# A recommender kernel on one core: a four-group layout, the history loop written out, and a reordered head

## The chip, the core and the metric

The kernel runs on one core of a Trainium2 chip. The core has five instruction streams: TensorE (PE) for matrix products, VectorE (DVE), ScalarE (ACT), GpSimd (POOL) and SyncE (SP). Here GpSimd issues gathers, and SP and ScalarE issue plain transfers. The metric is the device time of one execution in microseconds (us); less is better.

## The reference

The model scores 16384 users. Each has an item, a category and a history of 200 items.

```python
B, L, D = 16384, 200, 64
u = u_emb[user]; it = i_emb[item]; c = c_emb[cate]
h = i_emb[hist]                                   # L x B x D, a gather of 3.3 million rows
feat = concat([h, it, h - it, h * it], axis=-1)   # 256 features
a = dice(feat @ au_W1 + au_b1, au_alpha, axis=1)  # 36 units, statistics over the users of one l
w = a @ au_W2 + au_b2                             # one weight for each l and user
cur = sum(w * h, axis=0)                          # B x 64
z = concat([u, it, c, cur], axis=-1)
z = dice(z @ W1 + b1, alpha1, axis=0)             # 80 units
z = dice(z @ W2 + b2, alpha2, axis=0)             # 40 units
return z @ W3 + b3                                # 2 outputs

def dice(x, alpha, axis):
    p = sigmoid((x - mean(x, axis)) * rsqrt(var(x, axis) + 1e-8))
    return x * (p + alpha * (1.0 - p))
```

## The kernel before

**Splitting the product.** `feat @ au_W1` is taken apart by the four blocks of W1: a part that depends on the history row alone (`blk_h`), a part of the item alone (`blk_i`, with the bias), and the part of the product h * it (`blk_m`). The first is worked out once for all 100000 rows and stored beside them in DRAM (`table`, 128 floats a row); the second once for all users (`xi`). Only the third is a matrix product in the main work.

**Start.** 384 gathers of single columns of indices fetch the item, user and category rows into four `land` buffers (`fetch_one`, `keep_one`). Between them 49 blocks of table rows are loaded, transposed, multiplied and stored (`table_rows`, `table_store`). The order of `keep_one` and the blocks is written out by hand. After that the weights of the head are loaded, ten `land` buffers and both `hx` buffers are zeroed, and the ring of 12 `land` buffers starts.

**Main steps.** A step k handles 2048 users of one history position l; there are 8 steps to an l and 1600 in all. `manual_schedule` keeps the instructions of each engine in the order in which the code calls them. In step k:

- `fetch(k)` issues 16 indirect transfers on GpSimd (L202), each fetching 128 table rows of 512 bytes into `land[k % 12]`, and one transfer of `xi` on SP (L369).
- ScalarE works the gates of step k-10 (L448, L451) into the PSUM tile `pg`.
- `turn(k-1)` transposes both halves of the landed rows with four VectorE instructions (L377), and ScalarE copies one half to PSUM (L454).
- `hidden(k-2)` adds the product to the transposed table half (L390) and takes statistics (L392).
- ScalarE copies `xit` into `px` (L458); `product(k-1)` multiplies by the item (L384) and issues two TensorE products onto `px`.
- after the eighth step of an l, `moments` makes mean and variance of the whole l.
- `weigh(k-10)` multiplies gates and values, transposes, reduces, adds the two halves, weighs the rows and adds them to `cur` (L398 to L415).

The first calls of a run work on zeroed buffers, k-10 being negative. GpSimd refills `land[k % 12]` once `weigh(k-12)` has read it.

**The loop.** 24 positions l make one turn of `tc.For_i`, which runs seven times (192 steps a turn, 1344 steps); the last 32 positions (256 steps) are written out behind it:

```python
        rest_l = L % LPB + LPB
        with tc.For_i(0, L - rest_l, LPB) as l0:
            with tc.manual_schedule():
                for k in range(LPB * ND):
                    fetch_ids(k, l0, LPB + 1)
                    step(k)
```

In the part behind the loop, one matrix product a step prepares the head's first layer from the user, item and category rows (`base_of_layer1`), using the PSUM tile `pz`.

**The end.** After the last `fetch`, ten more steps drain the pipeline, with `layer1` of each of eight groups of users and its statistics between them. Then the head: for each group a sigmoid (L563), the scaling by alpha (L564) and a product (L565) make the dice, TensorE applies the second layer (L240), ScalarE saves its result with the bias (L595) and VectorE takes statistics (L525). After a second normalization the dice comes again, and 16 matrix products of the last layer (L604, two passes each) give the output.

Of the kernel before, what the change touches and what calls it, by code (L numbers as in the profile page):

```python
# [20 lines left out]
LPB = 24  # L21
LAND = 12
EARLY = 4
# [5 lines left out]
def din_kernel(  # L29
# [50 lines left out]

    parts = [(0, S), (S, A - S)]

# [3 lines left out]
    blk_h = once.tile([P, P], F32, name="blk_h")  # L86
    blk_i = once.tile([P, P], F32, name="blk_i")
    blk_m = const.tile([P, P], F32, name="blk_m")
    au_w = once.tile([P, 4, A], F32, name="au_w")
    au_bias = const.tile([P, 1], F32, name="au_bias")  # L90
    au_al = const.tile([P, 1], F32, name="au_al")
    au_1al = const.tile([P, 1], F32, name="au_1al")
    au_w2 = const.tile([P, 1], F32, name="au_w2")
# [4 lines left out]
    for e in range(2):  # L98
        rows = au_W1.rearrange("(g d) a -> d g a", d=D)[e * S : (e + 1) * S]
        for g in range(2):  # L100
            r = quarter(e, g)
            nc.sync.dma_start(au_w[r], rows)
            for q, (a0, n) in enumerate(parts):
                c, a = quarter(q, g, n), slice(a0, a0 + n)
                nc.vector.tensor_add(blk_h[r, c], au_w[r, 0, a], au_w[r, 2, a])
                nc.vector.tensor_sub(blk_i[r, c], au_w[r, 1, a], au_w[r, 2, a])
                nc.vector.tensor_copy(blk_m[r, c], au_w[r, 3, a])
    for g in range(2):
        for q, (a0, n) in enumerate(parts):
            r, a = quarter(q, g, n), slice(a0, a0 + n)  # L110
            nc.sync.dma_start(au_bias[r], col(au_b1)[a])
            nc.sync.dma_start(au_al[r], col(au_alpha)[a])
            nc.sync.dma_start(au_w2[r], au_W2[a])
# [11 lines left out]
    idx = [const.tile([P, NT], I32, name=f"idx{i}") for i in range(IDX)]  # L125
    stats = [const.tile([P, 2 * ND, nc.vector.BN_STATS_DIM], F32, name=f"st{i}") for i in range(2)]
    rstds = [const.tile([P, 1], F32, name=f"rs{i}") for i in range(2)]
    shifts = [const.tile([P, 1], F32, name=f"sh{i}") for i in range(2)]
    px, pz = (psum.tile([P, CD], F32, name=n) for n in ("px", "pz"))
# [6 lines left out]
    ucT = dram.tile([2, ND, P, CD], F32, name="ucT")  # L136
# [72 lines left out]
    def load_ids(t, ids):  # L209
        nc.sync.dma_start(t, ids.rearrange("(p n) -> p n", n=NT))  # L210

# [3 lines left out]
    def by_tile(t, i):  # L215

        return t[:, ts(i, CH)].rearrange("p (n t) -> p n t", t=S)

    def transpose(dst, rows, n=TD):

        for i in range(2):
            for e in range(2):
                nc.vector.transpose(  # L223
                    by_tile(dst[ts(e, D)], i)[:, :n], rows[ts(i, D), :n, ts(e, S)]
                )

    def transpose_back(rows, src, n=TD):

        for i in range(2):
            for e in range(2):  # L230
                nc.vector.transpose(
                    rows[ts(i, D), :n, ts(e, S)], by_tile(src[ts(e, D)], i)[:, :n]
                )

    def layer(dst, pairs, n=CH, onto=False):

        for i in range(2):
            cols = slice(i * CH, i * CH + n)
            for j, (lhsT, rhs) in enumerate(pairs):
                nc.tensor.matmul(  # L240
                    dst[:, cols], lhsT, rhs[:, cols],
                    start=(j == 0 and not onto), stop=(j == len(pairs) - 1),
                    skip_group_check=onto,
                )
# [13 lines left out]
    ids = [once.tile([P, NT], I32, name=f"ids{i}") for i in range(3)]  # L258
    for t, v in zip(ids, (r_item, r_user, r_cate)):
        load_ids(t, v)  # L260
# [11 lines left out]
    def table_rows(b):  # L272
# [11 lines left out]
        transpose(rT, tab, m)  # L284
        layer((px, pz)[b % 2], [(blk_h, rT)], n=m * S)
        tabs[b] = tab, m

    def table_store(b):
        n0, n = blocks[b]
        tab, m = tabs.pop(b)  # L290
        transpose_back(tab[:, :, D:], (px, pz)[b % 2], m)
        if n:
            nc.scalar.dma_start(grid_out[:, n0 : n0 + n], tab[:, :n])
        if m > n:
            nc.scalar.dma_start(table[P * per :], tab[:rest, n])
# [5 lines left out]
    def keep_one(j):  # L301
        c, k = j % ND, j // ND
        if k == 0:
            transpose(itT[:, c], land[j % EARLY])
            layer(ph, [(blk_i, itT[:, c])])
            t = pre.tile([P, CD], F32, tag="t", name="t")
            nc.scalar.activation(t, ph, AF.Identity, bias=au_bias)
            nc.scalar.dma_start(xi[c], t)
        else:
            t = pre.tile([P, CD], F32, tag="t", name="t")  # L310
            transpose(t, land[j % EARLY])
            nc.scalar.dma_start(ucT[k - 1, c], t)
# [22 lines left out]
    with ExitStack() as main:  # L335
# [15 lines left out]
        layer(px, [(blk_m, hx[0][:, 0])])  # L351
        nc.vector.bn_stats(stats[-1 % 2][:, 0, :], hx[0][:, 0, :CH])
        for c in range(1, 2 * ND):
            nc.vector.tensor_copy(stats[-1 % 2][:, c, :], stats[-1 % 2][:, 0, :])
        for i in range(2):
            nc.vector.memset(rstds[i], 0.0)
            nc.vector.memset(shifts[i], 0.0)
        nc.sync.dma_start(xit[-1 % XI], xi[ND - 1])

# [3 lines left out]
        def x_of(k):  # L363
            return land[k % LAND][:, :, D:]
# [6 lines left out]
        def turn(k):  # L371

            rows = land[k % LAND].rearrange("p n (s e c) -> p n s e c", s=2, e=2)
            for i in range(2):
                for e in range(2):
                    dst = hx[k % 2][ts(e, D), :, ts(i, CH)]
                    nc.vector.transpose(  # L377
                        dst.rearrange("p s (n t) -> p n s t", t=S), rows[ts(i, D), :, :, e]
                    )

        def product(k):

            hm = hx[k % 2][:, 0]
            nc.vector.tensor_mul(hm, ph, itT[:, k % ND])  # L384
            layer(px, [(blk_m, hm)], onto=True)

        def hidden(k):

            l, c = divmod(k, ND)
            nc.vector.tensor_add(x_of(k), by_row(px), by_row(hx[k % 2][:, 1]))  # L390
            for i in range(2):
                nc.vector.bn_stats(  # L392
                    stats[l % 2][:, 2 * c + i, :], x_of(k)[:, ts(i, TD // 2)]
                )

        def weigh(k):

            nc.vector.tensor_mul(by_row(pg), by_row(pg), x_of(k))  # L398
            yT = hx[k % 2][:, 0]
            nc.vector.transpose(yT, pg)  # L400
            r = small.tile([P, 2, TD], F32, tag="r", name="r")
            nc.vector.tensor_reduce(  # L402
                r, yT.rearrange("p (i n u) -> p i n u", i=2, u=S), mybir.AxisListType.X, ALU.add
            )
            r1 = small.tile([D, 2, TD], F32, tag="r1", name="r1")
            nc.vector.tensor_copy(r1, r[D:])  # L406
            w = ph[:, :TD]
            for i in range(2):
                nc.vector.scalar_tensor_tensor(  # L409
                    w[ts(i, D)], r[:D, i], au_bias2[:D], r1[:, i], ALU.add, ALU.add  # L410
                )
            c = k % ND
            rows = land[k % LAND][:, :, :D]
            nc.vector.tensor_mul(by_row(pg), rows, w.unsqueeze(2).to_broadcast([P, TD, D]))  # L414
            nc.vector.tensor_add(cur[:, ts(c, TD)], by_row(pg), cur[:, ts(c, TD)])  # L415

        def moments(l):

            i = l % 2
            mv = small.tile([P, 2], F32, tag="mv", name="mv")  # L420
            nc.vector.bn_aggr(mv, stats[i].rearrange("p c s -> p (c s)"))
            other = small.tile([P, 2], F32, tag="other", name="other")
            for q in range(2):
                for g in range(2):
                    nc.vector.tensor_copy(other[quarter(q, g)], mv[quarter(q, 1 - g)])  # L425
            total = small.tile([P, 2], F32, tag="total", name="total")
            nc.vector.tensor_add(total, mv, other)
            mean = small.tile([P, 1], F32, tag="mean", name="mean")
            nc.vector.tensor_scalar_mul(mean, total[:, 0:1], 0.5)
            dev = small.tile([P, 1], F32, tag="dev", name="dev")  # L430
            nc.vector.tensor_sub(dev, mv[:, 0:1], mean)
            half = small.tile([P, 1], F32, tag="half", name="half")
            nc.vector.tensor_scalar_mul(half, total[:, 1:2], 0.5)
            var = small.tile([P, 1], F32, tag="var", name="var")
            nc.vector.scalar_tensor_tensor(var, dev, dev, half, ALU.mult, ALU.add)  # L435
            scale_and_shift(mean, var, P, rstds[i], shifts[i])

        def step(k, last=None):
# [4 lines left out]

            if has(k):
                fetch(k)
            if has(k - 10):
                i = (k - 10) // ND % 2
                nc.scalar.activation(  # L448
                    by_row(pg), x_of(k - 10), AF.Sigmoid, bias=shifts[i], scale=rstds[i]
                )  # L450
                nc.scalar.activation(pg, pg, AF.Identity, bias=au_al, scale=au_1al)  # L451
# [201 lines left out]
```

## Time and profile before

| what | value |
|---|---|
| timed runs | 32784.65, 32846.29 and 32846.42 us; median 32846.29 us |
| the profiled execution | 32783.09 us, its span 32780.9 us |
| busy, share of the span | POOL 75%, DVE 78%, ACT 24%, PE 19% |
| gathers from `table` | 25600 of 943 ns |
| first gather, last gather | 9.83 us, 32514.03 us |
| data moved | 2667.86 MB, mean 81 GB/s |

The span reaches from the first to the last instruction of the profiled execution. A group line names the source line, engine and operation, then the tiles written and read, the number of instructions after "x", their busy time and mean duration in ns, and then the time that the engine stood idle before them, with what ended it. A timeline line gives start and duration in us, and in brackets the idle time before the instruction. A line of windows gives, for a stretch of the span, the busy time and the number of instructions of PE, its weight loads, DVE, ACT and POOL, then the granted TensorE clock, the share of the DMA engines and GB/s.

### The profile page before, as it was taken

To read this page: it belongs to the slowest core of one execution; us is meant where nothing else is said; L and a number is where in the kernel's file an instruction comes from. 1 tells how busy PE (TensorE), PEld (TensorE's weight loads), DVE (VectorE), ACT (ScalarE), POOL (GpSimd) and SP (SyncE) were. 2 spreads that over 40 slices of the span, in tenths; PEclk is the share of its full clock that TensorE was granted. 3 is DMA by queue.
4 is the path that set the end of the run, shared out by engine and by line. 5 is a ranking of instruction groups with operands and counts; after the bars stand their busy time and mean duration, and the time that the engine had idled before them with its cause. 6 is when DMAs were issued, how large, how long until landed. Compare 5 with 4: busy or idle time off the path is not lost. (4 is left out here: it accounts for less than half of the span.)

```text
span 32780.9 us, 100656 instructions
## 1 busy us (share of the span) xinstructions
PE 6366.6 (19%) x7006; PEld 2038.0 (6%) x7006; DVE 25567.4 (78%) x28797; ACT 7755.2 (24%) x7105; POOL 24515.6 (75%) x25991
## 2 busy tenths in 40 slices
PE   3111111111111111111111111111111112221112
PEld 0000000000000000000000000000000000000000
DVE  7777777777777777777777777777777777777777
ACT  1222222222222222222222222222222222222222
POOL 7777777777777777777777777777777777777775
PEclk5555555555555555555555555555555555555555
DMA  5222222222222222222222222222222223332222
GB/s 157 80 79 79 79 79 79 79 79 79 79 80 80 79 78 79 79 79 80 79 79 79 79 79 78 79 79 80 78 79 79 79 79 85 88 90 81 79 79 60
DMA packets 1214773, 2667.86 MB, mean 81 GB/s; under 512 B 551244, under 2 KB 577388, under 8 KB 1207916
## 3 DMA queue, kind: packets, MB, share of 16 engines
q0 software_dynamic: 831488, 1691.97, 19.6%
q1 hardware_dynamic: 372012, 906.09, 9.1%
q10 hardware_dynamic: 10560, 63.79, 0.5%
q14 instruction: 692, 5.67, 0.1%
q8 instruction: 21, 0.34, 0.0%
HBM read 2590.90 MB, written 69.16 MB: 81 GB/s over the span
## 5 line engine op out<-in xcount | busy, mean ns | idle before, releaser
L202 POOL DMA_INDIRECT land<-table,idx x25600 | 24152.2, 943 | 7872.6 <-issue 7703.8
L377 DVE STREAM_TRANSPOSE hx<-land 64x1024 f32<-64x1024 f32 x6404 | 7938.2, 1240 | 6360.3 <-DMA land<-table,idx 6218.5
L240 PE MATMUL px<-hx,blk_m 128*128 128x512 f32 x6408 | 5927.6, 1080 | 26007.0 <-DVE hx L384 25941.1
L448 ACT ACTIVATE pg<-land,sh,rs 128x1024 f32<-128x1024 f32 x1610 | 1943.8, 1207 | 12980.0 <-DVE cur L415 11593.3
L454 ACT COPY ph<-hx 128x1024 f32<-128x1024 f32 x1601 | 1627.6, 1017 | 10365.2 <-DVE hx L377 10362.2
L240 PEld LDWEIGHTS px<-hx,blk_m 128*128 128x128 f32 x6408 | 1880.1, 324 | 30022.8 <-issue 29846.4
L392 DVE BATCH_NORM_STATS2 st<-land 128x6 f32<-128x512 f32 x3204 | 2060.9, 685 | 55.0
L400 DVE STREAM_TRANSPOSE hx<-pg 128x1024 f32<-128x1024 f32 x1610 | 2011.7, 1250 | 55.2
L414 DVE TENSOR_TENSOR pg<-land,ph 128x1024 f32<-128x1024 f32 x1610 | 1977.8, 1228 | 55.0
L415 DVE TENSOR_TENSOR cur<-pg,cur 128x1024 f32<-128x1024 f32 x1610 | 1970.5, 1224 | 55.6
L402 DVE TENSOR_REDUCE r<-hx 128x32 f32<-128x1024 f32 x1610 | 1964.0, 1220 | 55.3
L390 DVE TENSOR_TENSOR land<-px,hx 128x1024 f32<-128x1024 f32 x1602 | 1961.6, 1224 | 49.5
L398 DVE TENSOR_TENSOR pg<-pg,land 128x1024 f32<-128x1024 f32 x1610 | 1968.8, 1223 | 2.7 <-ACT pg L451 2.5
L384 DVE TENSOR_TENSOR hx<-ph,itT 128x1024 f32<-128x1024 f32 x1601 | 1932.0, 1207 | 0.0
L451 ACT ACTIVATE pg<-pg,au_al,au_1al 128x1024 f32<-128x1024 f32 x1610 | 1895.0, 1177 | 54.3
L458 ACT COPY px<-xit 128x1024 f32<-128x1024 f32 x1601 | 1627.2, 1016 | 383.3 <-DVE land L390 381.1
L409 DVE SCALAR_TENSOR_TENSOR ph<-r,au_bias,r 64x16 f32<-64x16 f32 x3220 | 771.3, 240 | 114.8
L406 DVE COPY r<-r 64x32 f32<-64x32 f32 x1610 | 337.2, 209 | 55.0
L448 ACT ACT_TABLE_LOAD x209 | 268.1, 1283 | 452.6 <-DVE w1a L177 314.6
L249 ACT ACT_TABLE_LOAD x203 | 260.4, 1283 | 6.7 <-PE ph L555 3.2
L249 ACT ACTIVATE std<-var,eps 128x1 f32<-128x1 f32 x201 | 59.2, 295 | 475.2 <-DVE var L435 475.2
L425 DVE COPY other<-mv 32x2 f32<-32x2 f32 x804 | 155.6, 194 | 15.1
(122 smaller groups left out, 1885.8 us busy)
## 6 DMA issues: line engine op xcount, KB each, us to landing
xit<-xi SPq DMA_DIRECT2D x1601, 512.0 KB
land<-table,idx POOLq DMA_INDIRECT x25600
table<-tab ACTq DMA_DIRECT2D x48, 1024.0 KB
tab<-in_L_rec_i_emb SPq DMA_DIRECT2D x48, 512.0 KB
zt<-ucT SPq DMA_DIRECT2D x32, 512.0 KB
idx<-in_r_hist SPq DMA_DIRECT2D x200, 64.0 KB
ucT<-t ACTq DMA_DIRECT2D x16, 512.0 KB
zbase<-zt SPq DMA_DIRECT2D x10, 512.0 KB
```

Source lines behind the costliest of these rows:

```text
L202: nc.gpsimd.indirect_dma_start(out=dst[:, n, :], out_offset=None, in_=rows, in_offset=bass.IndirectOffsetOnAxis(ap=ids[:, n : n + 1], axis=0),
L240: nc.tensor.matmul(dst[:, cols], lhsT, rhs[:, cols], start=(j == 0 and not onto), stop=(j == len(pairs) - 1), skip_group_check=onto,)
L377: nc.vector.transpose(dst.rearrange("p s (n t) -> p n s t", t=S), rows[ts(i, D), :, :, e])
L384: nc.vector.tensor_mul(hm, ph, itT[:, k % ND])
L390: nc.vector.tensor_add(x_of(k), by_row(px), by_row(hx[k % 2][:, 1]))
L392: nc.vector.bn_stats(stats[l % 2][:, 2 * c + i, :], x_of(k)[:, ts(i, TD // 2)])
L398: nc.vector.tensor_mul(by_row(pg), by_row(pg), x_of(k))
L400: nc.vector.transpose(yT, pg)
L402: nc.vector.tensor_reduce(r, yT.rearrange("p (i n u) -> p i n u", i=2, u=S), mybir.AxisListType.X, ALU.add)
L414: nc.vector.tensor_mul(by_row(pg), rows, w.unsqueeze(2).to_broadcast([P, TD, D]))
L415: nc.vector.tensor_add(cur[:, ts(c, TD)], by_row(pg), cur[:, ts(c, TD)])
L448: nc.scalar.activation(by_row(pg), x_of(k - 10), AF.Sigmoid, bias=shifts[i], scale=rstds[i])
```

## The change

**A four-group layout.** The transposes of 32 by 32 blocks now keep the four groups of 32 partitions where they are, so that one instruction of 128 partitions takes the place of four. The features and units that no longer fit beside each other lie in two halves of the columns, and the first-layer product takes four matrix instructions for two. The weights of a user come out of one reduction, without the addition of two halves, and stay in PSUM. The two moments of an l are brought together over the four groups, in 32 partitions, and copied back to the others.

**x a step later.** `turn(k-1)` transposes straight into PSUM, and its product is issued at once, onto one of two PSUM tiles (`pxs`), into which ScalarE has copied `xit` in the step before. Gates, `weigh` and, in one step of eight, `moments` come next, and `hidden(k-2)` last. In the last `SPAN` = 144 steps only one of the two tiles is used, as the head's early work needs the other.

**No loop.** All 1600 steps are written out. The early work of the head starts 144 steps before the end and reads the item rows from DRAM too (`uicT`, three loads for two).

**Start.** The index loads come first in SP's queue. The zeroed statistics are taken 16 times instead of once with 15 copies.

**Head.** A second-layer result is saved two groups late (`keep2`), and in every second group ScalarE does the scaling by alpha.

The core of the diff:

```diff
-LPB = 24
 LAND = 12
+SPAN = 144
...
+    ids = [once.tile([P, NT], I32, name=f"ids{i}") for i in range(3)]
+    for t, v in zip(ids, (r_item, r_user, r_cate)):
+        nc.sync.dma_start(t, v.rearrange("(p n) -> p n", n=NT))
...
+    def halves(t, n=TD):
+        return t.rearrange("p (e n t) -> p e n t", e=2, t=S)[:, :, :n]
+    def of_rows(rows, n=TD):
+        return rows[:, :n].rearrange("p n (e c) -> p e n c", e=2)
+    def first_layer(dst, blk, rhs, n=CH, onto=False):
+        for q in range(2):
+            for e in range(2):
+                nc.tensor.matmul(
+                    dst[:, q * CH : q * CH + n], blk[:, e, q], rhs[:, e * CH : e * CH + n],
+                    start=(e == 0 and not onto), stop=(e == 1), skip_group_check=onto,
+                )
...
-        transpose(rT, tab, m)
-        layer((px, pz)[b % 2], [(blk_h, rT)], n=m * S)
+        nc.vector.transpose(halves(rT, m), of_rows(tab[:, :, :D], m))
+        first_layer(pxs[b % 2], blk_h, rT, n=m * S)
...
-        transpose_back(tab[:, :, D:], (px, pz)[b % 2], m)
+        nc.vector.transpose(of_rows(tab[:, :, D:], m), halves(pxs[b % 2], m))
...
-        layer(px, [(blk_m, hx[0][:, 0])])
-        nc.vector.bn_stats(stats[-1 % 2][:, 0, :], hx[0][:, 0, :CH])
-        for c in range(1, 2 * ND):
-            nc.vector.tensor_copy(stats[-1 % 2][:, c, :], stats[-1 % 2][:, 0, :])
+        for t in pxs:
+            first_layer(t, blk_m, hx[0][:, 0])
+        for q in range(2):
+            for c in range(ND):
+                nc.vector.bn_stats(stats[-1 % 2][:, q, c, :], hx[0][:, 0, :CH])
...
         def turn(k):
-            rows = land[k % LAND].rearrange("p n (s e c) -> p n s e c", s=2, e=2)
-            for i in range(2):
-                for e in range(2):
-                    dst = hx[k % 2][ts(e, D), :, ts(i, CH)]
-                    nc.vector.transpose(
-                        dst.rearrange("p s (n t) -> p n s t", t=S), rows[ts(i, D), :, :, e]
-                    )
+            rows = land[k % LAND]
+            hm, hw = hx[k % 2][:, 0], hx[k % 2][:, 1]
+            nc.vector.transpose(halves(ph), of_rows(rows[:, :, :D]))
+            nc.vector.tensor_mul(hm, ph, itT[:, k % ND])
+            nc.vector.transpose(halves(hw), of_rows(rows[:, :, D:]))
...
+            nc.vector.tensor_mul(halves(pg), halves(pg), x_of(k))
+            nc.vector.transpose(x_of(k), halves(pg))
+            r = ph[:, :TD]
+            nc.vector.tensor_reduce(
+                r, land[k % LAND][:, :, D:], mybir.AxisListType.X, ALU.add
+            )
...
+            nc.vector.scalar_tensor_tensor(
+                by_row(pg), r.unsqueeze(2).to_broadcast([P, TD, D]), au_bias2, rows,
+                ALU.add, ALU.mult,
+            )
...
+            for a in range(n):
+                nc.vector.tensor_copy(every[:, a], mv[ts(a, S)])
...
+            nc.scalar.activation(std, var, AF.Sqrt, bias=eps[:S], scale=1.0 / n)
...
+            for a in range(1, n):
+                nc.vector.tensor_copy(fac[ts(a, S)], fac[:S])
...
             if has(k):
                 fetch(k)
...
             if has(k - 1):
                 turn(k - 1)
-                nc.scalar.copy(ph, hx[(k - 1) % 2][:, 0])
+                if not single(k - 1):
+                    product(k - 1)
+            if has(k - 10):
+                if k % ND == 2:
+                    moments((k - 10) // ND)
+                gates(k - 10)
+                weigh(k - 10)
             if has(k - 2):
-                hidden(k - 2)
-            if has(k - 1):
-                nc.scalar.copy(px, xit[(k - 1) % XI])
+                hidden(k - 2, px_of(k - 2))
+            if has(k - 1) and single(k - 1):
+                preload(k - 1)
                 product(k - 1)
-            if has(k - 2) and (k - 2) % ND == ND - 1:
-                moments((k - 2) // ND)
-            if has(k - 10):
-                weigh(k - 10)
+            if has(k) and not single(k):
+                preload(k)
...
-        rest_l = L % LPB + LPB
-        with tc.For_i(0, L - rest_l, LPB) as l0:
-            with tc.manual_schedule():
-                for k in range(LPB * ND):
-                    fetch_ids(k, l0, LPB + 1)
-                    step(k)
-        K = rest_l * ND
+        K = L * ND
...
-        def dice(dst, t, p, factors, consts):
+        def dice(dst, t, p, factors, consts, c):
...
-            nc.vector.tensor_scalar(p[:n], p[:n], consts[2], consts[1], ALU.mult, ALU.add)
+            if c % 2:
+                nc.scalar.activation(
+                    p[:n], p[:n], AF.Identity, bias=consts[1], scale=consts[2]
+                )
+            else:
+                nc.vector.tensor_scalar(p[:n], p[:n], consts[2], consts[1], ALU.mult, ALU.add)
...
-                next(work, None)
+                if k > K - SPAN:
+                    next(work, None)
...
+            def keep2(c):
...
+            for c in range(ND + 2):
+                if c < ND:
+                    activated(c)
+                if c >= 2:
+                    keep2(c - 2)
```

## The prediction

> **What bounds the kernel now.** I read the page's busy table first, then its costliest groups, then the waits and the timeline of GpSimd alone, then the tail's timeline.
>
> ```profile
> PE 6366.6 (19%) x7006; PEld 2038.0 (6%) x7006; DVE 25567.4 (78%) x28797; ACT 7755.2 (24%) x7105; POOL 24515.6 (75%) x25991
> L202 POOL DMA_INDIRECT land<-table,idx x25600 | 24152.2, 943 | 7872.6 <-issue 7703.8
> L377 DVE STREAM_TRANSPOSE hx<-land 64x1024 f32<-64x1024 f32 x6404 | 7938.2, 1240 | 6360.3 <-DMA land<-table,idx 6218.5
> ```
>
> VectorE has the larger busy share, but it is not the bound: before its transposes it stands idle 6218 us, waiting for gathered rows. GpSimd's 25% of idle time is no slack: 7704 us of it follows nothing but the gather before ("issue"), about 0.30 us each. The windows give the period: 5000 us hold 3998 gathers inside the loop, 2000 us hold 1603 behind it.
>
> ```profile
> 10000.00:15000.00 5000.00, 925.70 (x1000) 293.36 (x1000) 3905.70 (x4368) 1194.29 (x1094) 3771.40 (x3998) 0.54 0.29 79
> 30000.00:32000.00 2000.00, 369.77 (x400) 117.37 (x400) 1564.93 (x1747) 477.65 (x438) 1511.68 (x1603) 0.54 0.29 79
> ```
>
> Single gathers start 1.248 us apart in both places. With 128 x 3 early ones there are 25984; at 1.248 us that is 32433 of 32781 us. A step is 16 gathers, 19.97 us. So the end is set by when GpSimd starts, by how often it stops, and by what follows its last gather. Its timeline shows where it stops:
>
> ```profile
> 9.83 1.09 POOL L202 DMA_INDIRECT land<-in_L_rec_i_emb,ids  x1 [9.37 <-DMA ids<-in_r_item]
> 539.53 0.94 POOL L202 DMA_INDIRECT land<-table,idx  x1 [9.45 <-issue]
> 12030.64 0.94 POOL L202 DMA_INDIRECT land<-table,idx  x1 [10.69 <-issue]
> 27402.62 0.94 POOL L202 DMA_INDIRECT land<-table,idx  x1 [3.36 <-issue]
> ```
>
> The brackets are idle time before the gather: the wait for the first indices; a stop at step 2; a turn of the loop; the loop's exit. After the last gather (32514.03) come 266 us: ten draining steps, then the head. One of the head's eight groups:
>
> ```profile
> 32715.54 1.11 ACT L595 ACTIVATE land<-pz,z2b 80x1024 f32<-80x1024 f32 x1 [8.43 <-PE pz L240]
> 32716.56 1.23 ACT L563 ACTIVATE land<-land,zshift,zrstd 128x1024 f32<-128x1024 f32 x1
> 32717.89 0.79 DVE L564 TENSOR_SCALAR land<-land,za1al,zaal 128x1024 f32<-128x1024 f32 x1
> 32718.72 1.23 DVE L565 TENSOR_TENSOR land<-land,land 128x1024 f32<-128x1024 f32 x1
> 32720.09 1.96 PE L240 MATMUL pg<-land,w2a 128*80 128x512 f32 x2 [4.58 <-DVE land L565]
> ...
> 32724.94 1.02 PE L240 MATMUL pg<-land,w2b 128*80 128x512 f32 x2
> 32726.00 1.11 ACT L595 ACTIVATE land<-pg,z2b 80x1024 f32<-80x1024 f32 x1 [8.22 <-PE pg L240]
> ```
>
> Nothing overlaps: ScalarE must save group c before its sigmoid of c+1, so a group takes 32726.00 - 32715.54 = 10.5 us, in which TensorE works 5.9 and idles 4.6.
>
> **What the Trainium skill says.** "TensorE: Matmul & The Clock Gate", Part 1 (the HAM clock gate): the array runs at half clock until about 3.4 us of sustained work. The trace agrees: in this group the matmul passes start 0.85 us apart at first, the last two (L240, w2b) 0.43 apart. "DMA: Bandwidth & Descriptors", SWDGE vs HWDGE vs iDMA: GpSimd builds gather descriptors in software, into rings that VectorE can lock away in its 2-port mode. No lock shows here: gathers keep 1.25 us whether VectorE works or idles. "ScalarE: Activation LUTs", What ACT_TABLE_LOAD costs: an ACTIVATE takes (N+335)/1.2 ns, 1132 for 1024 columns (trace 1207 and 1177), so as an estimate 706 for 512, and a table load 1283 (trace 1283).
>
> **The change, part by part.**
>
> *Main steps.* VectorE before, means of the groups: four L377 transposes 4.96, L384 1.21, L390 1.22, two L392 1.37, L398 1.22, L400 1.25, L402 1.22, L406 0.21, two L409 0.48, L414 1.23, L415 1.22: 15.6 us. After: three full transposes 3.75, six other full-width operations of 1.22, 7.3 (product, hidden's add, gate, reduce, weighing, sum), two statistics 1.37: 12.4. That saves 3.2 x 1600 = 5.1 ms of VectorE, and I count none of it: the cover is the gather stream of 19.97 us a step. TensorE doubles, from four passes to eight, 6.8 us even at half clock; ScalarE trades one copy for halved gates (four at about 0.65 for two at 1.2). Both are far below 19.97. One step in eight carries the moments, with about 7.5 us of small operations, two table loads and exposed gates in VectorE's order: near 20 us, but buffers allow it: in the trace L414, the last read of a land buffer, ends some 24 us before the gather that refills it, and weigh moves ahead of hidden in the step. SP issues the same xit loads, and the head's early work has three 512 KB reads a group for two; slices 35 and 36 of the page already hold such work (88, 90 GB/s against 79) and GpSimd did not stop there. Worth 0.
>
> *No loop.* Six turns: five cost 10.38 each over the period, the first (at 4332.68) 7.11, the exit 3.05: 62.1 us. No gather runs beside them, so they come off the end: **-62.1**. What replaces them is the form of the last 256 steps, straight code at the same 1.248 us. The price of 7 times as much straight code elsewhere: bound 0 (these steps) to +62 (as much as the turns); I take 0.
>
> *Start.* The indices are now SP's first loads instead of its 18th. Before, issue at 7.87, gather at 9.83; after, issue at 0.75, gather at about 2.7: **-7.1**. The affine selects wait in either place; now 22 gathers stand ahead of them, and VectorE's first table block starts near 35 us instead of 14, since it waits for their means. Covers: a block costs VectorE 2.5 us instead of 5.7, there are two per 20 us, and land is reused two steps late; 0 to +5, I take 0. The item's third store adds 8 x 0.5 MB beside a DMA share of 0.73; its cover is the same.
>
> *Step 2.* Gather 416 refills land2 after weigh(-10) has read it (L414 ends 538.8, gather 539.53). VectorE's chain starts at the last early landing (491.76) and moves with GpSimd. It changes by: 16 statistics at 0.63 for one and 15 copies (1.9), +8.2; turn with its product 6.2 to 3.7, -2.5; hidden and its statistics go behind weigh, -2.5; weigh up to its last read 5.6 to 4.9, -0.7. Together **+2.5**, a stop of about 12 us for 9.15; bounds 0 and +5. Later buffers have slack again (11 us by step 5 now).
>
> *Drain.* Step K 15.6 to 12.7, K+1 12.5 to 11.3 (now with 2.4 of waiting behind the px copy), K+2 12.4 to 16.7 (moments and exposed gates moved here): together +0.2. Seven steps with layer1 11.06 to 10.4, since gates (2.75) stay under statistics and transposes (4.1): **-4.4**; bounds -9 to +4.
>
> *Head.* Saving is two groups late, so TensorE runs on; every second scaling goes to ScalarE (1.2 there, 0.8 off VectorE). From the first sigmoid (32649.76) to the last pass (32736.35) it is 86.6 us. After: 5.4 as now, a first group 5.9 half cold, then warm passes: 8 x 0.43 = 3.5 each, 24.5: 35.8. ScalarE has about 27 us of work in it, VectorE 27, so they keep up, barely. **-50.8**; at half clock 8 x 0.85 = 6.8 a group, so 60.0 and -26.6. The last stage stays with TensorE: 32 passes 0.85 apart in 27.5 us (L604), whoever scales: 0.
>
> Sum: -62.1 - 7.1 + 2.5 - 4.4 - 50.8 = -121.9. The profiled execution took 32783.1 us (span 32780.9): **32661**. The timed runs were 32784.7, 32846.3 and 32846.4; the profiled one belongs to the first. The 62 us between them show in no trace.
>
> **Rivals.** (a) *The 62 us stay*: if two of three executions carry them for another reason than the turns, the median is 32723. For: two of three had them. Against: they equal the turns' total. (b) *A cold head*: TensorE stays at half clock, 32661 + 24 = 32685. For: L604 stays cold for 27 us. Against: every L240 group warms within 5 us. (c) *VectorE becomes the bound*, the slower side: its mean step passes 19.97 us. Place: the full-width operations on strided views (2x16x32), which the trace does not show. Price: 1.6 ms per us. It decides from 7.5 us a step more, 0.8 on each of nine operations, and would give, at one us beyond, 34260. Against: the strided L377 (1.240) costs no more than the plain L400 (1.250). (d) *The gather period grows*, through fetch or contention: 4.7 ns a gather eat the whole gain, 32783; the last 256 steps speak against it. That the scaling by turns does nothing is true already in the last stage.
>
> **How the numbers follow.** Forecast 0.60; (a) 0.20; (b), or drain and step 2 at their bad ends, 0.12; (c) 0.03; (d) 0.03, of which 0.01 slower; no turns saved because straight code stops as often, 32723, 0.02. A measurement can tell about 0.2%, 66 us of the median, so faster means below 32780: 0.94; same 0.02; slower 0.04. Range 32640 (drain and step 2 at their good ends) to 32745, just past (a) with part of (b).
>
> **What would show it.** Right: 25984 gathers still 1.248 us apart, the first near 2.7 us, one stop of about 12 us at step 2 and no other; VectorE busy near 20.5 ms with more idle behind gathers; last gather near 32448; head groups 3.5 us apart. Wrong: a gather mean above 0.943, stops ended by VectorE in the main steps, or a tail above 220 us.

## The result, and the profile after

In the first comparison the changed kernel took 32725.99 us (median of 7 runs, 32725.50 to 32727.81), the kernel before 32846.29 us (median of 7, 32784.65 to 32846.79): 120.3 us less, a ratio of 0.9966 with a 95% interval of 0.9955 to 0.9978. That is a third of a per cent, more than the 0.2% that the prediction took as measurable, and inside its range. The change is within 2 us of the sum of -121.9; the level is not: the point was 32661, and the median stands 65 us above it.

The profiled execution took 32725.5 us (span 32723.7). Its busy table and two of its costliest groups:

```profile
PE 9912.8 (30%) x13650; PEld 3856.9 (12%) x13650; DVE 20471.6 (63%) x21473; ACT 7128.0 (22%) x8734; POOL 24579.8 (75%) x25991
...
L212 POOL DMA_INDIRECT land<-table,idx x25600 | 24210.0, 946 | 7816.1 <-issue 7551.2
...
L389 DVE STREAM_TRANSPOSE ph<-land 128x1024 f32<-128x1024 f32 x1601 | 2013.6, 1258 | 10513.1 <-DMA land<-table,idx 10513.1
```

VectorE lost 5.1 ms of work and gained 4.3 ms of waiting for gathered rows ahead of its first transpose (6218 before, 10513 now). GpSimd's line is the surprise: the same 25600 gathers, 946 ns each where the first profile of the kernel before had 943. Start to start, 1.2506 us for 1.2482, in every part of the run; over 25983 periods the 2.4 ns are 62.6 us.

The timeline of GpSimd alone shows its stops (the bracket is the idle time before an instruction, and what released it):

```profile
2.95 1.09 POOL L212 DMA_INDIRECT land<-in_L_rec_i_emb,ids  x1 [2.50 <-DMA ids<-in_r_item]
4.35 0.95 POOL L212 DMA_INDIRECT land<-in_L_rec_i_emb,ids  x1 [0.30 <-issue]
5.60 6.38 POOL L212 DMA_INDIRECT land<-in_L_rec_i_emb,ids  x1 [0.30 <-issue]
12.28 0.94 POOL L212 DMA_INDIRECT land<-in_L_rec_i_emb,ids  x1 [0.30 <-issue]
...
528.33 0.94 POOL L212 DMA_INDIRECT land<-table,idx  x1 [0.30 <-issue]
540.51 0.94 POOL L212 DMA_INDIRECT land<-table,idx  x1 [11.23 <-issue]
```

The first gather starts at 2.95 us instead of 9.83. The stop at step 2 is there, with 11.23 us of idle time instead of 9.45. Nothing stops GpSimd after it: no turn, no exit. But the third gather lasts 6.38 us instead of 0.94, which no step of the prediction had. The VectorE timeline of that stretch has one long instruction, and the gather ends 0.9 us behind it:

```profile
4.21 6.88 DVE L129 MEMSET cur<- 128x8192 f32 x1 [1.66 <-issue]
```

In the head's middle, ScalarE's timeline answers to the 10.5 us groups of before:

```profile
32670.60 1.11 ACT L632 ACTIVATE land<-px,z2b 80x1024 f32<-80x1024 f32 x1 [0.39 <-PE px L253]
32671.61 1.23 ACT L591 ACTIVATE land<-land,zshift,zrstd 128x1024 f32<-128x1024 f32 x1
32672.87 1.24 ACT L593 ACTIVATE land<-land,zaal,za1al 128x1024 f32<-128x1024 f32 x1
32674.03 1.11 ACT L632 ACTIVATE land<-px,z2b 80x1024 f32<-80x1024 f32 x1
32677.46 1.11 ACT L632 ACTIVATE land<-pg,z2b 80x1024 f32<-80x1024 f32 x1 [2.32 <-PE pg L253]
```

Savings (L632) stand 3.43 us apart, which is eight TensorE passes 0.43 us apart. Sigmoid and scaling of a later group fit between two of them.

Between the two profiled executions, in us of span: turns and exit -62.1; first gather -6.9; third gather +5.4; affine selects -0.4; stop at step 2 +1.8; from the last gather to the head's first sigmoid -5.1 (135.7 to 130.6); middle of the head -50.8 (86.6 to 35.8); from the start of the last saving to the end -1.7 (44.5 to 42.8). Without the longer gathers that is -119.8; with their +62.6 it is -57.2, the difference of the spans (32723.7 - 32780.9).

### The profile page after: what moved, and what is told of

The parts are those of the page before. It is cut to its first block, busy times and chain, and to the rows that moved or that the text cites. A ratio compares the mean times of both kernels' runs of the same rounds, so it can differ in the third digit from the quotient of the medians.

```text
span 32723.7 us, 106467 instructions
## 1 busy us (share of the span) xinstructions
PE 9912.8 (30%) x13650; PEld 3856.9 (12%) x13650; DVE 20471.6 (63%) x21473; ACT 7128.0 (22%) x8734; POOL 24579.8 (75%) x25991
## 4 chain that ended last, share of the span: by engine, by line
POOL 51%; DVE 22%; issue 20%; DMA 7%; PE 0%; ACT 0%; DVEq 0%; POOLq 0%; SPq 0%; ACTq 0%
POOL land L212 51%; DMA land<-table,idx 6%; DVE pg L424 2%; DVE land L417 2%; DVE ph L389 2%; DVE ph L419 2%; DVE cur L428 2%; DVE hx L390 2%; DVE pg L416 2%; DVE hx L391 2%; DVE land L396 2%; DVE st L398 2%; DVEq L389 0%; PE px L649 0%; PE px L253 0%
## 5 line engine op out<-in xcount | busy, mean ns | idle before, releaser
L212 POOL DMA_INDIRECT land<-table,idx x25600 | 24210.0, 946 | 7816.1 <-issue 7551.2
L243 PE MATMUL px<-hx,blk_m 128*128 128x512 f32 x12824 | 9472.7, 907 | 22510.7 <-DVE hx L390 20520.8
L389 DVE STREAM_TRANSPOSE ph<-land 128x1024 f32<-128x1024 f32 x1601 | 2013.6, 1258 | 10513.1 <-DMA land<-table,idx 10513.1
L243 PEld LDWEIGHTS px<-hx,blk_m 128*128 128x128 f32 x12824 | 3682.6, 302 | 28298.3 <-issue 23381.2
L404 ACT ACTIVATE pg<-land,fac 128x512 f32<-128x512 f32 x3220 | 2508.7, 779 | 88.2 <-DVE cur L428 25.0
L409 ACT ACTIVATE pg<-pg,au_al,au_1al 128x512 f32<-128x512 f32 x3220 | 2419.1, 751 | 106.7
L424 DVE SCALAR_TENSOR_TENSOR pg<-ph,au_bias,land 128x1024 f32<-128x1024 f32 x1610 | 2081.8, 1293 | 57.2
L417 DVE STREAM_TRANSPOSE land<-pg 128x1024 f32<-128x1024 f32 x1610 | 2011.8, 1250 | 55.4
L419 DVE TENSOR_REDUCE ph<-land 128x16 f32<-128x1024 f32 x1610 | 1976.8, 1228 | 55.3
L391 DVE STREAM_TRANSPOSE hx<-land 128x1024 f32<-128x1024 f32 x1601 | 1975.3, 1234 | 0.0
L243 PE MATMUL px<-rT,blk_h 128*128 128x512 f32 (+1 forms) x392 | 219.7, 723 | 178.5 <-DVE rT L294 178.4
L212 POOL DMA_INDIRECT land<-in_L_rec_i_emb,ids x128 | 126.6, 989 | 41.1 <-issue 38.3
```

The lines of the kernel that those rows point to most:

```text
L212: nc.gpsimd.indirect_dma_start(out=dst[:, n, :], out_offset=None, in_=rows, in_offset=bass.IndirectOffsetOnAxis(ap=ids[:, n : n + 1], axis=0),
L243: nc.tensor.matmul(dst[:, q * CH : q * CH + n], blk[:, e, q], rhs[:, e * CH : e * CH + n], start=(e == 0 and not onto), stop=(e == 1), ski ...
L389: nc.vector.transpose(halves(ph), of_rows(rows[:, :, :D]))
L391: nc.vector.transpose(halves(hw), of_rows(rows[:, :, D:]))
L404: nc.scalar.activation(halves(pg)[:, q], x_of(k)[:, q], AF.Sigmoid, bias=facs[i][:, 1, q : q + 1], scale=facs[i][:, 0, q : q + 1],)
L417: nc.vector.transpose(x_of(k), halves(pg))
```

## The experiments

Three sessions followed. In one, on what is called the first chip here, the kernel before took 32784.57 us (median of 11), as in the shortest run of the first comparison; whether that comparison ran on the same chip is not known. In the other two, on a second chip, it took 36773.48 (median of 29) and 36901.71 us (25). Each kernel is compared with the kernel before of its own session. Numbers in brackets after a time are its ratio to that kernel and the 95% interval of the ratio. The tail is what follows the start of the last gather.

### Whose is the longer gather?

The kernel before and the changed kernel, as they are.

> The kernel before, profiled again. In its first profile gathers start 1.2482 us apart, in the profile of the changed kernel 1.2506, 62 us over 25984 gathers. Theory A (the period belongs to the execution, not to the change): either of the two periods can show here, and the time goes with it, 32784 or 32846 us. Rival B (the change lengthens each gather by 2.4 ns): 1.2482 here, whatever the time.

> The changed kernel again, beside the kernel before on one chip. Theory A: either period can show, 32661 to 32664 us with 1.2482 and 32723 to 32728 with 1.2506, and kernels that share a period differ by 120 us. Rival B: always 1.2506, about 32725. The tail behind the last gather is 209.3 us in both.

> The changed kernel beside the others on one chip, where the kernel before takes 32784 us if gathers start 1.2482 us apart. Theory A (the period is the execution's): 32664 us in that period, 120 less than before; 32726 in the longer one. Rival B (the change lengthens each gather by 2.4 ns): 32726 beside 32784 for the kernel before, 58 less.

*Measured.* Two page lines, each with a mean of one: the kernel before on the second chip (L202), and the changed kernel with another head (the experiment with all scaling on VectorE, below) on the first chip (L212):

```profile
L202 POOL DMA_INDIRECT land<-table,idx x25600 | 24213.4, 946 | 11719.4 <-issue 11479.2
```

```profile
L212 POOL DMA_INDIRECT land<-table,idx x25600 | 24153.5, 943 | 7812.4 <-issue 7386.1
```

The two values have changed places: 946 for the kernel before, 943 for the changed one. On the second chip the changed kernel itself had both: the commonest duration of a gather in its trace was 944 ns in one session and 947 in the next. And within the session on the first chip, one of the eleven runs of the kernel before took 32848.11 us, the ten others 32782.84 to 32785.69. **Theory A holds**: the duration belongs to the execution. Two executions of one of these kernels can lie 62 us apart for that alone; what chooses between the two values is open.

The times of the changed kernel on the second chip were 36675.87 (ratio 0.9973, 0.9963 to 0.9984) and 36742.80 us (0.9959, 0.9944 to 0.9974), 98 and 159 us below the kernel before. Neither the expected times nor the expected tail of 209.3 us (it was 223.0 and 232.6) came, for other limits hold there. GpSimd's timeline, first of the kernel before, then of the changed kernel:

```profile
20017.28 0.94 POOL L202 DMA_INDIRECT land<-table,idx  x1 [0.31 <-issue]
20020.92 0.95 POOL L202 DMA_INDIRECT land<-table,idx  x1 [2.70 <-issue]
```

```profile
20010.93 1.30 POOL L212 DMA_INDIRECT land<-table,idx  x1 [0.30 <-issue]
20012.53 1.11 POOL L212 DMA_INDIRECT land<-table,idx  x1 [0.30 <-issue]
20013.94 1.78 POOL L212 DMA_INDIRECT land<-table,idx  x1 [0.30 <-issue]
```

In the one, GpSimd waits before one gather in sixteen; in the other, six or seven gathers of each step are drawn out. Both come to 1.40 us a gather, 22.4 us a step, though their VectorE work is 15.6 and 12.4. For the kernel before, the trace shows what GpSimd waits for. Between its two gathers above, VectorE reads a `land` buffer for the last time:

```profile
20018.95 1.23 DVE L414 TENSOR_TENSOR pg<-land,ph 128x1024 f32<-128x1024 f32 x1 [1.15 <-issue]
```

This ends 0.74 us before the gather at 20020.92, the same distance as at the stop of step 2 in the first profile (538.8 and 539.53), and 838 of the 879 stops behind step 3 (starts over 2 us apart) end in this way. VectorE's wait for landed rows before L377, 6218 us in the first profile, is 48 us here; instead VectorE pauses between its own instructions, as for the 1.15 us in the bracket, with nothing that the profile names. So in the kernel before it is VectorE's order, drawn out by these pauses, that holds GpSimd back on this chip. What makes the pauses, and what draws out the gathers of the changed kernel, no record shows. Landings are not slower (a gather's last packet ends 1.19 us behind its instruction there, 1.25 in the first profile of the kernel before). Sizes are therefore taken from the first chip.

### The loop alone

```diff
-        rest_l = L % LPB + LPB
-        with tc.For_i(0, L - rest_l, LPB) as l0:
-            ...
+        rest_l = L
```

In the kernel before; the base of layer 1 is still computed beside the last 256 steps.

> The kernel before, with the loop alone written out; layout, start and head stay. Theory (a turn is 10.4 us in which GpSimd starts no gather, and nothing else is lost or gained): no stop at all after step 2, -62 us against the kernel before in the same period, 32722 or 32784. Rival (straight code of this length stops or slows GpSimd elsewhere, or lengthens its gathers): a change between -62 and 0, with gather starts more than 1.2482 us apart or new stops.

> The kernel before with the loop alone written out. Theory: -62 us against the kernel before in the same period, 32722 beside 32784, and no stop of GpSimd behind step 2. Rival (straight code stops or slows GpSimd elsewhere): less than 62, with stops or a longer period in the trace.

*Measured.* Both on the second chip: 36709.81 us, 63.7 less (0.9983, 0.9976 to 0.9990), and 36834.45 us, 67.3 less (0.9982, 0.9975 to 0.9989). The gain of 62 was expected, and both intervals hold it, though they are wide (37 to 88 and 41 to 92 us). It came even under that chip's own limit: the mean period behind step 3 went from 1.4017 to 1.3993 us, 62 us over 25551 gathers. But GpSimd stops at most steps on that chip, so that "no stop" could not be seen there, and the turns look different: it stops at a turn for about 23.5 us, start to start, where it was 11.6 in the first profile, and the steps right behind a turn take 20.0 us instead of 22.4. So the size agrees, while stops of 10.4 us over the period are seen in the first profile alone. On the first chip the loop was not tried alone; there the changed kernel's traces, with no stop behind step 2, are the evidence. The turns' 62.1 and the longer gathers' 62.6 have nothing in common but their size.

### The head's middle: later saving, or turns?

Two edits of the changed kernel. The first keeps all scaling on VectorE, the second saves each group at once:

```diff
-            if c % 2:
+            if False:
                 nc.scalar.activation(
```

```diff
-            for c in range(ND + 2):
-                if c < ND:
-                    activated(c)
-                if c >= 2:
-                    keep2(c - 2)
+            for c in range(ND):
+                activated(c)
+                keep2(c)
```

> The changed kernel with every scaling of the head's dice on VectorE. A middle group then costs VectorE 0.8 + 1.2 + 1.3 us and a fourth of the 2.0 for the rest, 3.8 us, for TensorE's 3.43. Theory F (the turns are what lets TensorE set the pace): the tail behind the last gather grows by about 3 us, 209.3 to 212 or 213. Rival G (the later saving alone does it): 209.3 within 0.5. Rival H (the turns cost more than they save): under 209.

> The changed kernel with each group of the head's middle saved at once, as before, the turns staying. Theory F and G: ScalarE's sigmoid of the next group waits behind the saving again, a group takes 10.5 us or a little more, and the tail grows by about 50 us, to 260. Rival H (the turns make the difference): it grows by less than 10.

*Measured.* One run each, 32668.14 and 32716.82 us. ScalarE's timeline, without turns and with saving at once:

```profile
32614.72 1.11 ACT L632 ACTIVATE land<-px,z2b 80x1024 f32<-80x1024 f32 x1 [1.19 <-PE px L253]
32618.16 1.11 ACT L632 ACTIVATE land<-pg,z2b 80x1024 f32<-80x1024 f32 x1 [2.32 <-PE pg L253]
32621.59 1.11 ACT L632 ACTIVATE land<-ph,z2b 80x1024 f32<-80x1024 f32 x1 [2.32 <-PE ph L253]
```

```profile
32607.34 1.11 ACT L632 ACTIVATE land<-px,z2b 80x1024 f32<-80x1024 f32 x1 [7.17 <-PE px L253]
32608.35 1.23 ACT L591 ACTIVATE land<-land,zshift,zrstd 128x1024 f32<-128x1024 f32 x1
32617.19 1.11 ACT L632 ACTIVATE land<-pg,z2b 80x1024 f32<-80x1024 f32 x1 [7.61 <-PE pg L253]
```

Without turns, savings still stand 3.43 us apart, and from first sigmoid to last saving it is 35.9 us for 35.8: rival G. VectorE's own instructions overlap by some 0.1 us at their seams, so a group costs it about 3.2 us (0.82 + 1.14 + 1.20 from start to start), and it keeps up alone. The tail was 213.1, near theory F's figure, but none of its 3.9 more lies in the middle, where theory F looked for it: 1.8 come before the first sigmoid, which the edit does not touch there, and 2.0 after the last saving, where the table load (1.28 us) for the next square root stands behind a wait instead of ahead of it. With saving at once the middle takes 87.3 us and the tail is 262.1: the whole gain returns. **The later saving is the gain; the turns add nothing to the middle.** What they do give, by this one run, is some 2 us behind it.

### How much VectorE work the gathers cover

```diff
-            nc.vector.transpose(halves(hw), of_rows(rows[:, :, D:]))
+            for _ in range(5):
+                nc.vector.transpose(halves(hw), of_rows(rows[:, :, D:]))
```

In turn of the changed kernel; with 9 in place of 5 in the second run.

> The changed kernel with four more full-width transposes in each step, 5.0 us of VectorE, the same result written again. Theory (the gather stream covers VectorE up to 20 us a step): about 17.4 us a step, 18.3 with the moments' share, no stop beyond those of the changed kernel and the same time within the spread of its runs. Rival (VectorE's order is as tight as its sum, because waits for landings and for TensorE lie in it): stops at one step in eight or in each, up to 8 ms more.

> The changed kernel with eight more full-width transposes in each step, 10.2 us of VectorE: about 22.6 us a step, 23.5 with the moments' share, for a gather stream of 20.0. Theory (VectorE is covered up to the stream's 20 us and sets the pace beyond): VectorE back to back, GpSimd stopped in each step, 1600 x 3.5 = 5.6 ms more, 38.3 ms. Rival (the slack is larger, since much of VectorE's order can lie in its waits): under 1 ms more.

*Measured.* 32683.00 us (5 runs; 0.9969, 0.9956 to 0.9982) with four more, on the first chip; 38591.59 us (one run) with eight more, on the second. The windows of 5000 us, with busy times of PE, PEld, DVE, ACT and POOL, for four, then eight:

```profile
10000.00:15000.00 5000.00, 1478.76 (x2008) 574.19 (x2008) 4385.76 (x4289) 1097.11 (x1348) 3779.14 (x4006) 0.63 0.27 79
```

```profile
10000.00:15000.00 5000.00, 1254.44 (x1696) 487.37 (x1696) 4749.91 (x4472) 926.78 (x1140) 3200.49 (x3393) 0.61 0.23 67
```

With four more, VectorE works 88% of the time and 5000 us still hold 4006 gathers, as many as at 1.248 us each: 7.9 ms of added work (28.39 ms busy for 20.47) cost nothing in the main steps. What it did cost, some 17 us, is where no gather covers it: the stop at step 2 grew from 12.2 to 17.3 us, start to start, a stop of 4.8 appeared at step 4, and the tail grew from 209.3 to 218.0. With eight more the order of the bounds turns: 3393 gathers in 5000 us, 23.6 us a step for 23.5 expected, 38.6 ms for 38.3. This ran on the chip where lighter kernels take 22.4 us a step anyway, so the time alone would prove little. The trace does: gathers last 943 ns, VectorE is busy for 95% of the window, GpSimd waits before each sixteenth gather, and 1548 of its 1625 stops behind step 3 end 0.74 us behind VectorE's last read of a `land` buffer.

### The third gather, and a better version

First cur zeroed by an addition at the same place; then a version without the work of the steps before the first, with cur zeroed elsewhere; then the same with eight pieces:

```diff
-    nc.vector.memset(cur, 0.0)
+    nc.vector.tensor_add(cur, zeros, zeros)
```

```diff
-        for k in range(-10, 0):
-            nc.vector.memset(land[k % LAND], 0.0)
         ...
+        nc.vector.memset(hx[0][:, 0], 0.0)
+        nc.vector.memset(cur, 0.0)
         ...
-                return last is None or j <= last
+                return 0 <= j <= last
```

```diff
-        nc.vector.memset(cur, 0.0)
         ...
+            for c in range(ND):
+                nc.vector.memset(cur[:, ts(c, TD)], 0.0)
```

The second also drops the sixteen statistics of zeros, the memsets of facs, most of those of hx, and the load and copy of `xit` for the step before the first.

> The changed kernel with cur zeroed at the same place by an addition of two zeros, about 9.7 us of VectorE for the memset's 6.88. In the changed kernel the third gather lasts 6.38 us for 0.94 while the memset runs. Theory C (the memset, in VectorE's faster mode, keeps GpSimd from writing its descriptors): the third gather takes 0.94, -5.4 us. Rival D (it is something else of the first gathers, a first use or a small load in the way): the third gather stays near 6 us, no change. Rival E (any long VectorE instruction does it): the stop grows to about 8 us.

> The changed kernel without the work of steps before the first (no zeroing of ten land buffers, no statistics of zeros, no weighing of them), and with cur zeroed at the start of the main stage instead of beside the third gather. Theory: the stop at step 2 (10.9 us over the period) and the third gather's 5.4 us go, so -16 us against the changed kernel; 32710 us where gathers start 1.2506 us apart and 32648 where they start 1.2482 apart. Rival: the stop comes back in another step, since the buffers are refilled in the same order and VectorE's first turn waits for the zeroing of cur; then -5 at most.

> The version without the work of steps before the first, cur now zeroed in eight pieces of 0.87 us right before step 0 (in the first such version its 6.9 us memset was still issued beside the third gather, which lasted 6.0 us). Theory C (a VectorE instruction of many microseconds holds the gather beside it until it ends; one of 0.87 us does not): every gather lasts 0.94, and 5 us go, 32649 us in the shorter period, 135 under the kernel before. Rival (a gather that early stops for another reason): the third gather stays near 6 us and the time at 32654.

*Measured.* The addition (36672.82 us; 0.9973, 0.9962 to 0.9983; second chip) moved the stop to the first gather and lengthened it, GpSimd and VectorE:

```profile
2.89 9.40 POOL L215 DMA_INDIRECT land<-in_L_rec_i_emb,ids  x1 [2.44 <-DMA ids<-in_r_item]
```

```profile
2.63 8.69 DVE L132 TENSOR_TENSOR cur<-zero 128x8192 f32<-128x8192 f32 x1
```

The third gather took 0.95, as theory C expected, but not for its reason: this was rival E, any long VectorE instruction. The addition started earlier than the memset had, beside the first gather, and this gather ends 0.97 us behind it. The second version (32654.44 us, 5 runs; 0.9961, 0.9947 to 0.9975; first chip) lost its stop at step 2 entirely (1.25 us start to start). It kept the other one: the memset, issued ahead of its place in the text, ran at 4.56, and the third gather lasted 6.00 us. In pieces, on the second chip, both were gone, although the pieces were issued just as early, GpSimd and VectorE:

```profile
6.22 0.95 POOL L211 DMA_INDIRECT land<-in_L_rec_i_emb,ids  x1 [0.30 <-issue]
```

```profile
6.06 0.91 DVE L592 MEMSET cur<- 128x1024 f32 x1
```

So it takes a long instruction, and a memset as such does no harm. This last version took 36737.98 us there (0.9957, 0.9944 to 0.9971). Its runs, 36728.51 to 36753.33, overlap those of the changed kernel (36739.41 to 36759.50), so the expected 16 us between them do not show on that chip, and on the first one it was not run. The version with one memset is the fastest measured on the first chip: 130 us below the kernel before, and some 10 below the changed kernel, which in the shorter period comes to about 32664 (32668.14 of the run without turns, less its 3.9 of longer tail; an estimate, not run).

## Why the prediction was right or wrong

**Bound: right.** The end is set by GpSimd's start, its stops and the tail. Saving 5.1 ms of VectorE gave nothing, and adding 7.9 ms took nothing in the main steps. Rival (c) put its threshold at 19.97 us a step. The two runs with added work bracket it: 17.5 us of VectorE work a step cost the main steps nothing, 22.4 set the pace (busy time over gathers in the two windows, on two chips).

**The gather's period: wrong, and nearly all of the 65 us of the level are this.** The step that failed is the choice between the forecast and rival (a). The sum was made on the profiled execution, whose 1.248 us was taken for a property of the kernel; rival (a), the 62 us stay, had 0.20, and "they equal the turns' total" was counted against it. The equality was chance. By their times, six of seven runs of the kernel before and all seven of the changed one carried 2.4 ns more a gather than the profiled execution of the kernel before. The text had itself said that the 62 us show in no trace; a profile of one execution could not settle which of the two periods the median would have, and two of three times already lay in the longer one. Its sign of a wrong forecast, a gather mean above 0.943, did appear, and the experiments show that it was no doing of the change. Rival (d) thus had the right symptom and the wrong cause. That the medians differ by the sum, 120.3 for 121.9, is luck twice over. Both medians lie in the longer period; had only one of them, the difference would have been about 59 us (32784.65 less 32725.99) or, as an estimate, 182 (32846.29 less the 32664 worked out above). And in the sum a missed loss (5.4, below) is nearly made up by smaller items that came out better than forecast (step 2, the drain, the end).

**No loop: right.** -62.1 forecast; in the trace no stop is left behind step 2, and the loop alone gave 64 and 67 on the second chip, under another limit. The doubt that straight code stops as often has nothing for it.

**Start: -7.1 forecast, -1.5 net.** The first gather moved by 6.9. The term that was missed is the third gather's +5.4: "no lock shows here" was read from main steps whose longest VectorE instruction is about 1.3 us, while the 6.88 us memset of cur had ended as the first gather began and now ran beside it. Moving the gathers forward moved them into it. Whoever moves work has to look at what already runs at the new place. The affine selects and the later first block cost nothing, as taken.

**Step 2: +2.5 forecast, +1.8 measured.** The stop of 12.2 us start to start is the one forecast, and dropping the work that feeds it removed it whole.

**Drain: -4.4 forecast, -5.1. Head: -50.8 forecast, -50.8.** First sigmoid to last saving took 35.8 us, to the tenth. The part given to the turns, that they let the engines keep up, was not needed. A further -1.7 after the last saving was not forecast: the square root's table load now runs while VectorE still does statistics, and it is gone again without the turns. **Cold head (b): no.** The first group's passes stand 0.85 us apart for about 5 us, the others 0.43. Of the 3.4 us that the prediction quotes for the warming, "the trace agrees" said too much: the traces show about 5 us here, and in the kernel before the last stage's 32 passes stayed 0.85 apart through 27.5 us of unbroken work. The estimate of 706 ns for a halved gate was low as well: L404 and L409 took 779 and 751. The formula quoted from the Trainium skill is for an instruction that reads one value for each partition beside its data, the bias; these read two, bias and scale. Nothing hung on it, as ScalarE was busy for 22% of the span.

**The signs.** VectorE busy 20.5 ms: right (20.47). First gather near 2.7: 2.95. Last gather near 32448: 32514.4, late by the longer period, 62.6, and the third gather, 5.4. Groups 3.5 apart: 3.43. Tail under 220: 209.3.

## What to carry to other kernels

Before summing savings in microseconds, look at the single times: if they lie in two groups, ask which group the profiled execution is of, and state the level for both. Ask of each saving whether the engine that it frees is the one that the end waits for; here, on the first chip, 5.1 ms of VectorE were worth nothing and 62 us of loop turns, 50 us of a saving placed two groups later and 11 us of needless first steps were worth all. When the first gather is moved earlier, check each long VectorE instruction at the new place, and cut it into pieces.

## What the runs showed of the hardware

- One program's gathers last 943 or 946 ns on the mean, constant through an execution where nothing else draws them out, and the difference is worth 62 us of 32.7 ms.
- A long VectorE instruction (6.88 us memset, 8.69 us addition) held a gather until 0.9 us behind its own end. The Trainium skill, "SBUF — State Buffer", Who interferes with whom, says that an instruction that takes the port pair shared by VectorE and GpSimd blocks the other engine for its whole length. It does not name a memset among them for this chip, and of additions like this it infers that they do not stall the writing of descriptors; measured, both held a gather. Nor was every gather beside a long instruction held: the gather before the blocked one ran 4.35 to 5.30 us, inside the same memset, unharmed, and so did one of 0.95 us at 500.81 inside a memset of 1.76 us at 500.49. What tells them apart is open.
- A second chip ran the kernel before and the changed one some 12% slower, at 22.4 us a step. In the first, VectorE pauses between its instructions (1.15 us before the one shown); in the second, gathers last 1056 and 1047 ns on the mean. No record names the cause of either.
